# Reordering the opening of a fused cross-attention and feed-forward kernel, and moving small VectorE operations to GpSimd

## The chip, the cores and the metric

The kernel runs on one core of a Trainium2 chip. The metric is the device time of one execution in microseconds (us), lower is better. A core has TensorE (matrix products, called PE in the profile; its weight loads are PEld), VectorE (DVE), ScalarE (ACT), GpSimd (POOL) and SyncE (SP, which here only issues transfers). Each engine works through its own queue in the order in which the program wrote it, and waits on semaphores for the others. PSUM is the memory that TensorE writes; SBUF holds everything else on the chip.

## The reference

`x` has 2048 tokens of 256 numbers, the context 1601 tokens of 192; there are 16 heads of 64, and one learned "null" key and value is put in front of the context's.

```python
x = x + attention(layernorm(x), context, mask, ...)
x = x + ffn(layernorm(x), ...)

def attention(t, context, mask, g_norm, null_kv, Wq, Wkv, Wout, g_out):
    q = (layernorm(t) * g_norm) @ Wq
    k, v = split(context @ Wkv)                    # 16 heads
    k, v = concat(null_k, k), concat(null_v, v)    # 1602 keys
    sim = where(mask, q @ k.T / 8, -max)
    return layernorm(softmax(sim) @ v @ Wout) * g_out

def ffn(h):                                        # weights are +1 or -1
    h = 2 * relu(s0 * (concat(h, -h) @ sign(k0)))  # 512 -> 1024
    h = 2 * relu(s1 * (h @ sign(k1)))              # 1024 -> 1024
    return s2 * (h @ sign(k2))                     # 1024 -> 256
```

## The kernel before

**Units.** Attention is worked in 32 units: 8 pairs of heads (`p`) by 4 blocks of 512 tokens (`b`), with `u` counting them from 0 to 31. The 1602 keys are cut into 13 tiles of 128 (`KC`), the last of which holds 66 (`KLAST`). In a unit, `exps` computes for each key tile the scores of both heads on TensorE (L414), which ScalarE turns into exponentials (L440). In between, `max_chunk` computes the scores of the *next* unit in a faster number format (L373), and VectorE takes their row maxima (L376); twelve chunks of up to 512 keys, and one short chunk `REST` for the last 66 keys (L357, L360). `max_combined` (L381) joins the maxima, `max_turned` transposes them on TensorE (L386) and spreads them on VectorE (L388). They are subtracted in the next unit's first two key tiles (L438).

**Sums of the exponentials.** GpSimd adds the exponentials of the 13 tiles to `acc`, first tiles 1 to 7 while they come (L689, L691), then tile 0, which holds the 66 last keys, and tiles 8 to 12 (L699). Before tile 0 is added or used, ScalarE scales its rows from 64 on with `spent` (L697), a count of masked keys that `masked_counted` works out in unit 0 on VectorE (L400 to L404). TensorE multiplies the exponentials with the values (L447), tile 0 last. In the next unit ScalarE copies one element of the finished `acc` (L680) ahead of the third exponential. So the exponentials from there on, which reuse the buffers, need no further wait for GpSimd.

**Norms of the tokens.** `input_root` takes the statistics of a block on VectorE (L79, L80) and the root on ScalarE (L508); `input_normed` takes the reciprocal (L512), and with `beside` lets ScalarE subtract and scale in eight operations (L145, L146). Root and exponential need different tables on ScalarE, so each change between them is an ACT_TABLE_LOAD. `input_turned` transposes on TensorE and multiplies with the norm weights `gn_sb` (L526 to L530). Blocks 0 and 1 are done in the opening, 2 and 3 at the end of units 0 and 1 (L710 to L712), after the scaling and the sums have been issued.

**The opening** (L548 to L646) is written out by hand: transfers on three queues (SP, ScalarE, GpSimd), idle products on the identity, the first tokens, then for head pair 0 the keys in four chunks (`first_keys`: L230, L231, and L222 on VectorE), the values in four groups of two halves (`first_values`, copied by ScalarE at L295), the queries (`project_q`) and the maxima of unit 0. All of them take PSUM from two pools with two banks each; `slot` takes them from the two pools in turn, so a request is served when the tile that was taken four requests earlier has been read. `keys_stepped` (L272) is GpSimd's: it replaces key tiles by differences, since scores are summed up in PSUM from tile to tile.

**Other small work.** In unit 3 VectorE derives the signs and scales of the feed-forward part from `s0`, `s1`, `s2` (L748 to L752); they are first used in unit 28. In units 1 to 3 it also masks the context (`context_masked`, L407). The feed-forward part follows unit 31.

The order on each engine is the order of the program's text: both parts stand in `tc.manual_schedule()`.

Of the kernel before, what the change touches and what calls it, by code (L numbers as in the profile page):

```python
# [19 lines left out]
M = 1601  # L20
KEYS = M + 1
CD = 192
HEADS, DH = 16, 64
# [15 lines left out]
def xattn_ffn(ctx, tc, x, ctxT, mask, g_norm, null_kv, wq, wkv, wout, g_out, k0, k1, k2, s0, s1, s2, out):  # L39
    nc = tc.nc  # L40
# [3 lines left out]
    sp = ctx.enter_context(tc.tile_pool(name="stats", bufs=2))  # L44
# [10 lines left out]
    x_sb = cp.tile([128, NB * 4, D], F32, name="x_sb")  # L55
    y_sb = cp.tile([128, NB * 4, D], F32, name="y_sb")
    gout_sb = cp.tile([128, D], F32, name="gout_sb")
    s_sb = cp.tile([128, 3], F32, name="s_sb")
# [89 lines left out]
    with ExitStack() as att:  # L148
# [22 lines left out]
        def load_pair(p):  # L171
            wq_t = pp.tile([128, 2, 128], F32, tag="wq", name=f"wq_{p}")
            wa_t = pp.tile([128, 2, 128], F32, tag="wa", name=f"wa_{p}")
            wb_t = pp.tile([128, 2, 128], F32, tag="wb", name=f"wb_{p}")
            wo_t = lp.tile([128, D], F32, tag="wo", name=f"wo_{p}")
            both = wkv.rearrange("r (k w) -> r k w", k=2)[:, :, ts(p, 128)]
            nc.sync.dma_start(out=wa_t, in_=both[0:128])
            nc.sync.dma_start(out=wb_t[:64], in_=both[128:CD])
            if p == 0:

                nc.vector.memset(wb_t[64:], 0.0)
            else:
                nc.sync.dma_start(out=wb_t[64:], in_=both[128:CD])
            nc.sync.dma_start(out=wq_t, in_=wq[:, ts(p, 128)].rearrange("(c r) w -> r c w", c=2))
            if p > 0:
                nc.sync.dma_start(out=wo_t, in_=wout[ts(p, 128), :])
            weights[p] = (wq_t, wa_t, wb_t, wo_t)
# [36 lines left out]
        def first_keys(n, get):  # L224

            kT, _, kr = pairs[0]
            start, w = CHUNKS[n]
            keys = ds(start, w)
            ps = get(f"psk_0_{n}")
            nc.tensor.matmul(ps[:, 0, :w], weights[0][1][:, 0, :], ctx_a[:, keys], start=True, stop=False)  # L230
            nc.tensor.matmul(ps[:, 0, :w], weights[0][2][:, 0, :], ctx_b[:, keys], start=False, stop=True)  # L231

            relative(kT, ps[:, 0, :w], keys)
            if n == 3:
                nc.vector.memset(kT[:, KEYS:], 0.0)
            if n == 0:
                nc.scalar.copy(kr[:, keys], kT[:, keys])
            else:
                nc.gpsimd.tensor_copy(kr[:, keys], kT[:, keys])
# [138 lines left out]
        def max_combined(p, b):  # L378

            cols = mcol.rearrange("p (j c) -> p c j", j=2)[:, 0:4, :]  # L380
            nc.vector.tensor_reduce(cols, maxima[p, b], AX.X, ALU.max, negate=True)  # L381
# [16 lines left out]
        def masked_counted():  # L398

            nc.vector.tensor_reduce(spent, keep[:, 1:], AX.X, ALU.add)  # L400
            nc.vector.tensor_scalar(spent, spent, float(M), None, ALU.subtract)
            nc.vector.tensor_tensor(spent, spent, ident[:, KLAST : KLAST + 1], ALU.mult)
            for row in range(64, KLAST):
                nc.vector.tensor_tensor(spent, spent, ident[:, row : row + 1], ALU.add)  # L404

        def context_masked(part, start, end):
            nc.vector.tensor_tensor(part[:, start:end], part[:, start:end], keep[:, start:end], ALU.mult)  # L407
# [94 lines left out]

        def input_root(b):
            mv = stats(x_sb[:, ts(b, 4), :], 4, f"x{b}")
            r = sp.tile([128, 4], F32, tag="rstd", name=f"rstd_x{b}")
            nc.scalar.activation(r, mv[:, :, 1], AF.Sqrt, bias=eps2_sb, scale=1.0 + EPS)  # L508
            return mv, r

        def input_normed(b, mv, r, beside=False):
            nc.vector.reciprocal(r, r)  # L512
            if beside:
                centred_beside(y_sb, x_sb, mv, r, b)
                return
            for j in range(4):
                centred(y_sb[:, 4 * b + j, :], x_sb[:, 4 * b + j, :], mv, r, j)

        def input_turned(b, get=flex):

            pt = get(f"xT_{b}")
            pts = (pt, (get if b == 0 else spare)(f"xT_{b}_1") if b in (0, 2) else pt)
            for j in range(4):
                for c in range(2):
                    nc.tensor.transpose(pts[c][:, c, ts(j, 128)], y_sb[:, 4 * b + j, ts(c, 128)], ident)
            nc.scalar.mul(xnT[:, b, 0, :], pts[0][:, 0, :], gn_sb[:, 0:1])  # L526
            if b == 1:
                nc.scalar.mul(xnT[:, b, 1, :], pts[1][:, 1, :], gn_sb[:, 1:2])
            else:
                nc.vector.tensor_scalar_mul(xnT[:, b, 1, :], pts[1][:, 1, :], gn_sb[:, 1:2])  # L530
# [7 lines left out]
        def load_x(b):  # L538
            nc.sync.dma_start(out=x_sb[:, ts(b, 4), :], in_=x[ts(b, 512), :].rearrange("(c p) d -> p c d", p=128))

        def load_context(engine, n):
            at, w = CHUNKS[n]
            skip = 1 if n == 0 else 0
            engine.dma_start(out=ctx_a[:, ds(at + skip, w - skip)], in_=ctxT[0:128, ds(at + skip - 1, w - skip)])
            engine.dma_start(out=ctx_b[:64, ds(at + skip, w - skip)], in_=ctxT[128:CD, ds(at + skip - 1, w - skip)])


        nc.gpsimd.memset(keep[:, 0:1], 0)  # L548
        nc.gpsimd.dma_start(out=keep[:, 1:], in_=mask.partition_broadcast(128))
        for t in range(4):  # L550
            (nc.sync, nc.scalar)[t % 2].dma_start(out=x_sb[:, t, :], in_=x[ts(t, 128), :])
        load_context(nc.scalar, 0)
        load_pair(0)
        load_context(nc.sync, 1)
        load_x(1)
        load_context(nc.sync, 2)
        load_context(nc.sync, 3)
        nc.sync.dma_start(out=weights[0][3], in_=wout[ts(0, 128), :])
# [7 lines left out]
        nc.vector.memset(ctx_a[:, KEYS:], 0.0)  # L566
        nc.vector.memset(ctx_b[:64, KEYS:], 0.0)
        nc.vector.memset(ones, 1.0)
        make_identity(nc, ident)
        nc.gpsimd.dma_start(out=gn_sb, in_=g_norm.rearrange("(c p) -> p c", p=128))  # L570
        for j in range(2):
            nc.gpsimd.dma_start(out=nullk[ts(j, DH), :], in_=null_kv[0].rearrange("(p o) -> p o", o=1))
        nc.gpsimd.memset(mcol_u8[0:1, 0:1], 1)
        nc.gpsimd.dma_start(out=mcol_u8[1:128, 0:1], in_=mask[0:127].rearrange("(p o) -> p o", o=1))
        nc.gpsimd.dma_start(
# [20 lines left out]
        input_normed(0, *xn)  # L596

        idle = slot("idle")
        for _ in range(16):
            nc.tensor.matmul(idle[:, 0, :128], ident, ident, start=True, stop=True)  # L600
        input_turned(0, slot)
        first_keys(0, slot)
        project_q(0, 0, slot)

        xn = input_root(1)
        first_keys(1, slot)
        input_normed(1, *xn, beside=True)

        nc.gpsimd.tensor_copy(kept[:, : KC - 1], mcol_u8[:, : KC - 1])
        nc.gpsimd.tensor_copy(kept[:KLAST, KC - 1 : KC], mcol_u8[:KLAST, KC - 1 : KC])  # L610

        max_chunk(0, 0, 0, slot)
        max_chunk(0, 0, 3, slot)
        first_keys(2, slot)
        max_chunk(0, 0, 6, slot)
        max_chunk(0, 0, 9, slot)
        first_values(0, 0, slot)
        first_values(0, 1, slot)

        nc.scalar.activation(warm, eps_sb, AF.Exp)  # L620
        max_chunk(0, 0, 1, slot)
        max_chunk(0, 0, 4, slot)
        first_keys(3, slot)
        keys_stepped(0)
        first_values(1, 0, slot)
        max_chunk(0, 0, 7, slot)
        first_values(1, 1, slot)
        max_chunk(0, 0, 10, slot)
        max_chunk(0, 0, 2, slot)
        input_turned(1, slot)  # L630
        first_values(2, 0, slot)
        max_chunk(0, 0, REST, slot)
        first_values(2, 1, slot)
        max_chunk(0, 0, 5, slot)
        first_values(3, 0, slot)
        max_chunk(0, 0, 8, flex)
        project_q(0, 1, spare, 0)
        max_chunk(0, 0, 11, flex)
        project_q(0, 1, spare, 1)
        max_combined(0, 0)  # L640

        odd = spare("sT_0_0_1")
# [6 lines left out]
        with tc.manual_schedule():  # L649
            for u, (p, b) in enumerate(units):  # L650
# [40 lines left out]
                        nc.gpsimd.tensor_tensor(acc, acc, es[k], ALU.add)  # L691
                if nxt is not None:
                    max_combined(*nxt)
                if u == 0:
                    masked_counted()

# [7 lines left out]
                if u == len(units) - 2:  # L704
# [2 lines left out]
                    norm_end(0, y_sb, y_sb, beside=True)  # L707

                    nc.scalar.activation(warm, eps_sb, AF.Exp)
                if u < 2:  # L710
                    input_normed(u + 2, *input_root(u + 2), beside=True)
                    nc.scalar.activation(warm, eps_sb, AF.Exp)  # L712
                if u == 0:


                    nc.sync.dma_start(out=ctx_b[64:, 1:KEYS], in_=ctxT[128:CD, :])


# [24 lines left out]
                    context_masked(ctx_b, 0, 1024)  # L743
                if u == 3:
                    context_masked(ctx_b, 1024, KEYS)


                    nc.vector.tensor_scalar(sgn, s_sb[:, 0:2], 0.0, None, ALU.is_ge)  # L748
                    nc.vector.tensor_scalar(sgn, sgn, 2.0, -1.0, ALU.mult, ALU.add)
                    nc.vector.tensor_tensor(s_sb[:, 0:2], s_sb[:, 0:2], sgn, ALU.mult)  # L750
                    nc.vector.tensor_scalar(s_out, s_sb[:, 0:1], s_sb[:, 1:2], 8.0, ALU.mult, ALU.mult)
                    nc.vector.tensor_tensor(s_out, s_out, s_sb[:, 2:3], ALU.mult)  # L752
                if p + 1 < NP and b in (1, 2):
                    round_k(p + 1, b - 1)
                avs = lp.tile([128, 512], F32, tag="avs", name=f"avs_{p}_{b}", bufs=1)
# [172 lines left out]
```

## Time and profile before

| what | before |
|---|---|
| median of 3 runs | 1285.53 us (1283.4 to 1285.76) |
| the profiled execution | 1286.19 us |
| its span, first to last instruction | 1284.4 us |
| mean granted TensorE clock | 0.994 |
| busy: TensorE, VectorE, ScalarE, GpSimd | 1264.9, 768.3, 716.8, 1005.9 us |
| first exponential of unit 0 | starts at 38.65 us |
| copy that awaits the sums, units 1, 2, 3, 4 | 76.70, 111.15, 144.67, 184.26 us |

A line of the timeline gives the start in us from the first instruction, the duration in us, the engine, the line of the program, the operation, output and inputs by name with their shapes, and how many instructions are merged in it. In brackets stands the idle time of the engine just before and what ended it. A line of the waits reads: who waited, for whom, us in total, how often, the longest. A line of the windows gives for a stretch of time its length, the busy time of PE, PEld, DVE, ACT and POOL, then the granted clock of TensorE (1.00 is full), the share in which the transfer engines were busy, and GB/s.

### The profile page before, as it was taken

The page shows a single profiled execution, that of the slowest core. Times are in us where ns is not written, and L with a number is a line of the kernel's source. Part 1 is how long each engine was busy: PE and PEld are TensorE (multiplying, and loading weights), DVE is VectorE, ACT ScalarE, POOL GpSimd, SP SyncE. Part 2 cuts the span into 40 slices and gives each one's busy share as a digit, 9 for nine tenths or more (in the row PEclk, how much of TensorE's full clock was granted, in tenths as well). Part 3 has the DMA queues.
Part 4 walks back from the last instruction along what each step waited for, and adds up shares of the span by engine and source line. Part 5 has one row for each costly group of instructions (what it writes and reads, how often), then busy time and mean ns, then how long its engine had stood idle before and what let it go on. Part 6 is the DMA issues. An engine that isn't in the chain of part 4 may idle for free.

```text
span 1284.4 us, 19605 instructions
## 1 busy us (share of the span) xinstructions
PE 1264.9 (98%) x8336; PEld 651.5 (51%) x8336; DVE 768.3 (60%) x831; ACT 716.8 (56%) x974; POOL 1005.9 (78%) x505
## 2 busy tenths in 40 slices
PE   8999989999999999999999999999999999999998
PEld 6334444444444444444444444444444433788887
DVE  6778676656665666565666566656666783644432
ACT  3676645666566656666666666666666666422120
POOL 5688978899889988999889988998899999801100
PEclk9999989999999999999999999999999999999999
DMA  5100000000000000000000000000000010000000
GB/s 145 23 1 5 1 1 13 5 1 1 14 5 1 1 14 5 1 1 14 5 1 1 1 13 5 1 1 5 1 17 1 1 42 1 1 12 6 17 17 17
DMA packets 16169, 13.40 MB, mean 10 GB/s; under 512 B 2689, under 2 KB 15553, under 8 KB 16081
## 3 DMA queue, kind: packets, MB, share of 16 engines
q1 hardware_dynamic: 14944, 11.02, 3.1%
q8 instruction: 65, 1.06, 0.3%
q10 hardware_dynamic: 656, 0.79, 0.2%
q0 software_dynamic: 480, 0.34, 0.2%
q14 instruction: 24, 0.19, 0.0%
HBM read 10.04 MB, written 2.10 MB: 9 GB/s over the span
## 4 chain that ended last, share of the span: by engine, by line
PE 87%; POOL 7%; DVE 2%; ACT 2%; DMA 1%; issue 1%; SPq 0%; DVEq 0%; POOLq 0%; ACTq 0%
PE sT L414 26%; PE av L447 23%; PE ps L810 11%; PE max L373 6%; PE po L460 4%; PE psq L215 4%; POOL acc L699 4%; POOL acc L691 3%; PE ps L841 2%; PE psv L316 2%; PE psk L247 2%; PE psv L328 1%; PE sT L438 1%; PE den L471 1%; PE psk L252 1%; DMA x_sb<-in_x 1%
## 5 line engine op out<-in xcount | busy, mean ns | idle before, releaser
L376 DVE TENSOR_REDUCE mx<-max 128x2 f32<-128x1024 f32 x384 | 444.0, 1219 | 90.2 <-PE max L373 86.4
L699 POOL TENSOR_TENSOR acc<-acc,e 128x1024 f32<-128x1024 f32 x192 | 473.3, 2465 | 16.8 <-ACT e L697 1.8
L440 ACT ACTIVATE e<-sT 128x1024 f32<-128x1024 f32 x416 | 424.9, 1023 | 88.0 <-PE sT L438 45.3
L414 PE MATMUL sT<-qT,kT 64*128 64x512 f32 x1664 | 445.0, 609 | 5.1 <-ACT e L440 5.0
L691 POOL TENSOR_TENSOR acc<-acc,e 128x1024 f32<-128x1024 f32 x160 | 378.9, 2368 | 12.5
L447 PE MATMUL av<-e,v 128*32 128x512 f32 x3328 | 363.6, 592 | 0.0
L373 PE MATMUL max<-kr,qr 64*128 64x512 f32 x768 | 280.8, 719 | 0.8 <-DVE mx L376 0.8
L447 PEld LDWEIGHTS av<-e,v 128*32 128x32 f32 x3328 | 107.6, 110 | 237.5 <-issue 229.9
L414 PEld LDWEIGHTS sT<-qT,kT 64*128 64x128 f32 x1664 | 134.6, 186 | 135.8 <-ACT e L440 123.5
L689 POOL TENSOR_TENSOR acc<-e,e 128x1024 f32<-128x1024 f32 x32 | 75.6, 2361 | 76.5 <-ACT e L440 76.5
L373 PEld LDWEIGHTS max<-kr,qr 64*128 64x128 f32 x768 | 76.7, 188 | 88.9 <-DVE mx L376 66.2
L489 ACT COPY aoT<-r 32x256 f32<-32x256 f32 x224 | 90.2, 403 | 33.5 <-DVE r L483 31.2
L756 ACT COPY avs<-av 128x512 f32<-128x512 f32 x32 | 18.7, 585 | 145.0 <-PE av L447 145.0
L388 DVE TENSOR_TENSOR mT<-mt,pick 128x512 fp32r<-128x512 f32 x32 | 22.1, 691 | 116.9 <-PE mt L386 116.9
L490 DVE TENSOR_TENSOR aoT<-avs,aoT 128x512 f32<-128x512 f32 x28 | 26.9, 961 | 94.3 <-ACT aoT L489 94.3
L810 PE MATMUL ps<-h0hi,w 128*128 128x512 f32 x256 | 79.5, 392 | 0.0
L810 PE MATMUL ps<-h0lo,w 128*128 128x512 f32 x256 | 78.9, 390 | 0.0
L124 POOL TENSOR_TENSOR y_sb<-y_sb,gout_sb 128x256 f32<-128x256 f32 x12 | 9.3, 776 | 86.0 <-DVE y_sb L91 86.0
L216 ACT ACTIVATE qr<-psq 128x512 fp32r<-128x512 f32 x32 | 19.1, 597 | 95.0 <-PE psq L215 92.3
L798 ACT ACTIVATE h1hi<-ps 128x1024 fp32r<-128x1024 f32 x16 | 16.4, 1027 | 98.9 <-PE ps L810 98.9
L215 PE MATMUL psq<-xnT,wq 128*128 128x512 f32 x124 | 59.0, 599 | 2.0 <-ACT xnT L526 2.0
L460 PE MATMUL po<-wo,aoT 128*128 128x256 f32 x256 | 60.6, 380 | 0.0
(170 smaller groups left out, 1199.4 us busy)
## 6 DMA issues: line engine op xcount, KB each, us to landing
out_x<-o SPq DMA_DIRECT2D x7, 256.0 KB, 2.1
x_sb<-in_x SPq DMA_DIRECT2D x3, 512.0 KB, 9.1
wa<-in_wkv SPq DMA_DIRECT2D x8, 128.0 KB, 3.0
wq<-in_wq SPq DMA_DIRECT2D x8, 128.0 KB, 2.2
wo<-in_wout SPq DMA_DIRECT2D x8, 128.0 KB, 2.1
xnT<-in_k SPq DMA_DIRECT2D x1, 1024.0 KB, 5.5
wb<-in_wkv SPq DMA_DIRECT2D x15, 64.0 KB, 2.5
ctx_a<-in_ctxT SPq DMA_DIRECT2D x2, 256.0 KB, 7.3
```

The lines of the kernel that those rows point to most:

```text
L215: nc.tensor.matmul(ps[:, 0, :], weights[p][0][:, c, :], xnT[:, b, c, :], start=c == 0, stop=c == 1)
L373: nc.tensor.matmul(ps[:, j, :w], qr[rows, ts(t, 128)], kr[rows, ds(start, w)], start=True, stop=True)
L376: nc.vector.tensor_reduce(maxima[p, b][:, t, :, c], ps[:, :, :w], AX.X, ALU.max)
L414: nc.tensor.matmul(ps[:n, j, :], kT[rows, ds(128 * KEY_TILES[k], n)], qT[rows, :], start=k < 2, stop=k >= 2, skip_group_check=k >= 2,)
L440: nc.scalar.activation(e, ps, AF.Exp)
L447: nc.tensor.matmul(av[ts(i, 32), 0, :], v[:n, KEY_TILES[k], ts(i, 32)], e[:n, i // 2, :], start=k == 1, stop=k == 0, tile_position=(0, 32 ...
L460: nc.tensor.matmul(pv[:, t, :], aoT[:, ts(t, 128)], weights[p][3], start=True, stop=True)
L489: nc.scalar.copy(aoT[ds(64 * j + 32 * rows, 32), ts(h, 256)], r[ds(64 * j + 32 * h, 32), :])
L689: nc.gpsimd.tensor_tensor(acc, es[1], es[2], ALU.add)
L691: nc.gpsimd.tensor_tensor(acc, acc, es[k], ALU.add)
L699: nc.gpsimd.tensor_tensor(acc, acc, es[k], ALU.add)
L810: nc.tensor.matmul(ps[:, f, :], w(c)[:, ts(2 * g + f, 128)], parts[part][:, c, :], start=i == 0, stop=i == len(steps) - 1,)
```

## The change

It has six parts.

1. GpSimd builds the identity first and issues the transfers of the norm weights `gn_sb` and the null key `nullk` ahead of the mask's.
2. SP loads the second block of tokens ahead of the second chunk of the context.
3. The statistics of block 1 are split: two of its four tiles ahead of the first keys, two behind them; its root goes behind `project_q`, and the rest of its norm behind the first two chunks of maxima. The idle products go from 16 to 11.
4. In the opening, chunks of maxima come ahead of the keys of chunks 1 to 3, and the short chunk `REST` comes last.
5. In units 0 and 1 the norm of blocks 2 and 3 comes ahead of the count of masked keys and of the scaling of tile 0, and so ahead of GpSimd's sums of tiles 0 and 8 to 12.
6. The count's small steps, three instead of four, and the five operations on signs and scales go from VectorE to GpSimd, the latter from unit 3 to unit 4.

```diff
         def masked_counted():
             nc.vector.tensor_reduce(spent, keep[:, 1:], AX.X, ALU.add)
-            nc.vector.tensor_scalar(spent, spent, float(M), None, ALU.subtract)
-            nc.vector.tensor_tensor(spent, spent, ident[:, KLAST : KLAST + 1], ALU.mult)
+            nc.gpsimd.tensor_scalar(spent, spent, float(M), ident[:, KLAST : KLAST + 1], ALU.subtract, ALU.mult)
             for row in range(64, KLAST):
-                nc.vector.tensor_tensor(spent, spent, ident[:, row : row + 1], ALU.add)
+                nc.gpsimd.tensor_tensor(spent, spent, ident[:, row : row + 1], ALU.add)
...
         nc.gpsimd.memset(keep[:, 0:1], 0)
+        make_identity(nc, ident)
+        nc.gpsimd.dma_start(out=gn_sb, in_=g_norm.rearrange("(c p) -> p c", p=128))
+        for j in range(2):
+            nc.gpsimd.dma_start(out=nullk[ts(j, DH), :], in_=null_kv[0].rearrange("(p o) -> p o", o=1))
         nc.gpsimd.dma_start(out=keep[:, 1:], in_=mask.partition_broadcast(128))
...
         load_pair(0)
+        load_x(1)
         load_context(nc.sync, 1)
-        load_x(1)
...
         idle = slot("idle")
-        for _ in range(16):
+        for _ in range(11):
             nc.tensor.matmul(idle[:, 0, :128], ident, ident, start=True, stop=True)
         input_turned(0, slot)
+        mv = stats(x_sb[:, 4:6, :], 2, "x1")
         first_keys(0, slot)
+        stats(x_sb[:, 6:8, :], 2, "x1", mv)
         project_q(0, 0, slot)
-        xn = input_root(1)
-        first_keys(1, slot)
-        input_normed(1, *xn, beside=True)
+        r = input_scale(1, mv)
...
         max_chunk(0, 0, 0, slot)
         max_chunk(0, 0, 3, slot)
-        first_keys(2, slot)
+        input_normed(1, mv, r, beside=True)
+        first_keys(1, slot)
         max_chunk(0, 0, 6, slot)
+        first_values(0, 0, slot)
         max_chunk(0, 0, 9, slot)
-        first_values(0, 0, slot)
         first_values(0, 1, slot)
         nc.scalar.activation(warm, eps_sb, AF.Exp)
         max_chunk(0, 0, 1, slot)
         max_chunk(0, 0, 4, slot)
+        first_keys(2, slot)
+        max_chunk(0, 0, 7, slot)
+        first_values(1, 0, slot)
+        max_chunk(0, 0, 10, slot)
+        first_values(1, 1, slot)
+        max_chunk(0, 0, 2, slot)
         first_keys(3, slot)
         keys_stepped(0)
-        first_values(1, 0, slot)
-        max_chunk(0, 0, 7, slot)
-        first_values(1, 1, slot)
-        max_chunk(0, 0, 10, slot)
-        max_chunk(0, 0, 2, slot)
+        max_chunk(0, 0, 5, slot)
         input_turned(1, slot)
         first_values(2, 0, slot)
-        max_chunk(0, 0, REST, slot)
+        max_chunk(0, 0, 8, slot)
         first_values(2, 1, slot)
-        max_chunk(0, 0, 5, slot)
-        first_values(3, 0, slot)
-        max_chunk(0, 0, 8, flex)
+        max_chunk(0, 0, 11, flex)
         project_q(0, 1, spare, 0)
-        max_chunk(0, 0, 11, flex)
+        first_values(3, 0, flex)
         project_q(0, 1, spare, 1)
+        max_chunk(0, 0, REST, flex)
         max_combined(0, 0)
...
                 if nxt is not None:
                     max_combined(*nxt)
+                if u < 2:
+                    input_normed(u + 2, *input_root(u + 2), beside=True)
+                    nc.scalar.activation(warm, eps_sb, AF.Exp)
                 if u == 0:
                     masked_counted()
...
-                if u < 2:
-                    input_normed(u + 2, *input_root(u + 2), beside=True)
-                    nc.scalar.activation(warm, eps_sb, AF.Exp)
...
-                    nc.vector.tensor_scalar(sgn, s_sb[:, 0:2], 0.0, None, ALU.is_ge)
-                    nc.vector.tensor_scalar(sgn, sgn, 2.0, -1.0, ALU.mult, ALU.add)
-                    nc.vector.tensor_tensor(s_sb[:, 0:2], s_sb[:, 0:2], sgn, ALU.mult)
-                    nc.vector.tensor_scalar(s_out, s_sb[:, 0:1], s_sb[:, 1:2], 8.0, ALU.mult, ALU.mult)
-                    nc.vector.tensor_tensor(s_out, s_out, s_sb[:, 2:3], ALU.mult)
+                if u == 4:
+                    nc.gpsimd.tensor_scalar(sgn, s_sb[:, 0:2], 0.0, None, ALU.is_ge)
+                    nc.gpsimd.tensor_scalar(sgn, sgn, 2.0, -1.0, ALU.mult, ALU.add)
+                    nc.gpsimd.tensor_tensor(s_sb[:, 0:2], s_sb[:, 0:2], sgn, ALU.mult)
+                    nc.gpsimd.tensor_scalar(s_out, s_sb[:, 0:1], s_sb[:, 1:2], 8.0, ALU.mult, ALU.mult)
+                    nc.gpsimd.tensor_tensor(s_out, s_out, s_sb[:, 2:3], ALU.mult)
```

`input_scale(b, mv)` is new: it takes the two lines of `input_root` that take the root of the variances on ScalarE.

More of the change, by code (lines that the diff above doesn't have):

```diff
@@ L500, in divided, with input_scale @@
             return aoT
+        def input_scale(b, mv):
+            r = sp.tile([128, 4], F32, tag="rstd", name=f"rstd_x{b}")
+            nc.scalar.activation(r, mv[:, :, 1], AF.Sqrt, bias=eps2_sb, scale=1.0 + EPS)
+            return r
         def input_root(b):
             mv = stats(x_sb[:, ts(b, 4), :], 4, f"x{b}")
-            r = sp.tile([128, 4], F32, tag="rstd", name=f"rstd_x{b}")
-            nc.scalar.activation(r, mv[:, :, 1], AF.Sqrt, bias=eps2_sb, scale=1.0 + EPS)
-            return mv, r
+            return mv, input_scale(b, mv)
         def input_normed(b, mv, r, beside=False):
@@ L568, in xattn_ffn @@
         nc.vector.memset(ones, 1.0)
[L569 to L572, printed above, removed]
         nc.gpsimd.memset(mcol_u8[0:1, 0:1], 1)
```

## The prediction

> **What bounds the kernel now.** I read the page's totals first, then who waited for whom in the first units, and then each engine's timeline there, because the change touches only the opening and the units 0 to 4.
>
> ```profile
> PE 1264.9 (98%) x8336; PEld 651.5 (51%) x8336; DVE 768.3 (60%) x831; ACT 716.8 (56%) x974; POOL 1005.9 (78%) x505
> ...
> PE psv L316 <- DVE mT L388: 3.9, 1, 3.9
> PE psq L215 <- ACT xnT L526: 2.0, 1, 2.0
> ```
>
> TensorE is busy 98% of the span, so a gain can only come out of its few holes. The second view (waits of TensorE between 38 and 250 us) names the two of over 1 us behind the opening. The first, 3.9 us, is at the end of unit 3. This is VectorE's timeline there:
>
> ```profile
> 168.02 2.31 DVE L748 TENSOR_SCALAR sgn<-s_sb 128x2 f32<-128x2 f32 x1
> 170.37 0.17 DVE L749 TENSOR_SCALAR sgn<-sgn 128x2 f32<-128x2 f32 x1
> 170.58 2.19 DVE L750 TENSOR_TENSOR s_sb<-s_sb,sgn 128x2 f32<-128x2 f32 x1
> ...
> 173.05 2.13 DVE L752 TENSOR_TENSOR s_out<-s_out,s_sb 128x1 f32<-128x1 f32 x1
> 175.10 0.68 DVE L388 TENSOR_TENSOR mT<-mt,pick 128x512 fp32r<-128x512 f32 x1
> ```
>
> Three tiny operations take over 2 us each while GpSimd adds, and the turned maxima (L388) stand behind them. The second hole is ScalarE's, at the end of unit 0; then come GpSimd's sums:
>
> ```profile
> 52.40 1.02 ACT L440 ACTIVATE e<-sT 128x1024 f32<-128x1024 f32 x1 [0.28 <-PE sT L414]
> 57.20 1.15 ACT L697 ACTIVATE e<-e,spent 64x1024 f32<-64x1024 f32 x1 [3.78 <-DVE spent L404]
> 58.37 1.28 ACT L508 ACT_TABLE_LOAD   x1
> ...
> 66.68 0.69 ACT L526 ACTIVATE xnT<-xT,gn_sb 128x512 f32<-128x512 f32 x1
> ```
>
> ```profile
> 58.49 14.54 POOL L699 TENSOR_TENSOR acc<-acc,e 128x1024 f32<-128x1024 f32 x6 [1.79 <-ACT e L697]
> 77.97 2.37 POOL L689 TENSOR_TENSOR acc<-e,e 128x1024 f32<-128x1024 f32 x1 [4.94 <-ACT e L440]
> ```
>
> The reader is to see the order on ScalarE: last exponential, scaling of the last key tile (L697), then the norm of later tokens. GpSimd's last six sums start with the tile that L697 scales. In the next unit a one-element copy on ScalarE (L680) waits for the last of them, and every later exponential is queued behind it:
>
> ```profile
> 76.70 0.17 ACT L680 COPY seen<-acc 1x1 f32<-1x1 f32 x1
> 76.87 1.02 ACT L440 ACTIVATE e<-sT 128x1024 f32<-128x1024 f32 x1
> ```
>
> The sums ended at 58.49 + 14.54 = 73.03, so L680 had 3.67 us to spare. In unit 2 it stands at 111.15 and the sums (16.40 us from 92.65) ended at 109.05: 2.10 us to spare. Last, the clock and the opening:
>
> ```profile
> 17.46:20.88 3.42, 2.03 (x10) 1.01 (x10) 3.42 (x7) 2.84 (x8) 0.87 (x3) 1.00 1.09 313
> 20.88:24.29 3.41, 3.41 (x17) 2.81 (x15) 2.27 (x3) 1.68 (x5) 0.65 (x2) 0.50 0.18 46
> ```
>
> ```profile
> 11.96 0.75 DVE L222 SCALAR_TENSOR_TENSOR kT<-psk,nullk,keep 128x512 f32<-128x512 f32 x1 [1.08 <-PE psk L231]
> 14.93 0.43 DVE L79 BATCH_NORM_STATS2 st_x<-x_sb 128x6 f32<-128x256 f32 x1 [2.22 <-DMA x_sb<-in_x]
> ```
>
> A stretch of 3.4 us in which TensorE was busy only 2.03 us is followed by one at a granted clock of 0.50. And VectorE, which works in order, sat 2.22 us until the second tokens landed.
>
> **The change part by part.** The profiled execution took 1286.19 us (span 1284.4), 0.66 over the median of the three runs. Sums are made on its rows.
>
> *Unit 3's five operations.* They leave VectorE for GpSimd one unit later. In unit 3 TensorE transposed the maxima at 168.16; 0.37 later (so in unit 2) L388 could start: 168.53. From L388 to the next L680 an undisturbed unit of this kind takes 316.31 - 307.33 = 8.98 us, so L680 would stand at 177.51, and stands at 184.26: 6.75 us, 3.90 of it the hole, the rest work at clock 0.50 (174.5 to 181.3). GpSimd's sums of unit 3 end at 177.59, so 0.1 comes back: **-6.65** (ends -3.9, if only the hole counts, and -6.75). On GpSimd the five cost about 0.21 us each (the 128x4 addition of the opening, L589), 1.05 us; that they are behind unit 4's sums and ahead of unit 5's, where GpSimd idled 3.1 us, covers it. If that cover were gone it would be 1.05 us once. What reads them runs in unit 28 and after.
>
> *Unit 0: the norm ahead of the scaling.* Also the count of masked keys ends on GpSimd: three operations of 0.2 us for VectorE's 0.15, 0.70 and twice 0.16. In the new order ScalarE loads its table at 53.45 instead of idling. VectorE's statistics (2.2 us from 53.98) end at 56.2, root, reciprocal and mean follow by 56.9, eight ScalarE operations as at 92.79 to 96.67 (3.88) end at 60.8, the table back and its first use at 62.2. Only then the scaling, 62.2 to 63.35; the count (reduction 1.8 from 56.9, then GpSimd's 0.6) is ready at 59.5 and no longer matters. TensorE wants the scaled tile at 62.95 and waits 0.45. Its transposes and their copy follow with 0.7 of idling, and the projection L215 starts at 66.15 instead of 67.43; with no drop of the clock its 3.95 us (1.72 + 1.35 + 0.88, as around 210) put the first scores of unit 1 at 70.1 instead of 73.16. That is a gain of 3.06, and it isn't kept: GpSimd's six sums start at 63.45 instead of 58.49 and end at 78.0. L680 would be ready at 76.70 - 3.06 = 73.64 and waits 4.4 us. Behind it are the exponentials, behind them TensorE's scores, two tiles on. Unit 1's third exponential starts at 78.17, where it started at 76.87: **+1.3**, less 0.2 that TensorE wins back by steps of 1.09 instead of 1.13.
>
> *The clock after that wait.* TensorE idles some 4.4 us. Holes of 2.20 us (64.8 to 67.43) and 3.90 cost 1.78 (5.73 instead of 3.95 us up to the scores) and 2.85 more at half clock. How much falls on work depends on where the hole lies against the 3.4 us stretches: between 0 and 2.85, taken as **+2.0**, between the two rows.
>
> *Unit 1: the same order.* Here ScalarE did not idle ahead of L697, so nothing is gained. The scaling, at 89.46, goes behind the norm: 98.1 to 99.25. GpSimd's six sums, which began at 92.65, begin at 99.3 and at unit 0's 14.54 end at 113.85; L680 of unit 2 was at 111.15: **+2.7**, however late unit 1 runs as a whole. Less 0.3 won back, and **+1.8** of clock (ends 0 and 2.85; taken at the 2.20 us hole's 1.78, the nearest). TensorE itself wants unit 1's scaled tile at 100.1, after 99.25. In unit 2 the scaling stays where it was and GpSimd's delay dies: its sums end at about 148.8, L680 comes at 152.
>
> [...]
>
> *The opening.* The norm weights land earlier (10.03 before), but the query projection also waits for its weights, which landed at 11.03: nothing. Five idle products fewer (ten matmuls of 0.213 us) let the transposes run when the tokens are ready, but the first keys' matmuls wait for weights that land at 9.8: nothing. The mask, issued behind the identity and three small transfers on GpSimd, lands about 2 us later than 7.88, before the first keys at 11.96. On SP the second tokens pass two context transfers. Before, those tokens took 2.18 us behind what preceded them (12.73 to 14.91); behind the query weights (11.03) they land at about 13.2, and the context at about 14.9, where the second keys now need it at 17.2. But VectorE now has half the statistics *ahead of* the first keys' L222: 13.2, two pairs of 0.53 to 14.3, L222 to 15.1 (before: 12.7), its copy on ScalarE to 15.75, the scaled queries behind it to 16.35. The maxima's matmuls start then (15.23 before), their reductions at 16.95 (17.84 before). Then in turn: two reductions 2.28, reciprocal and mean 0.25, eight ScalarE operations 3.88, the copy of the first values 0.58 (queued behind them), at 24.0; keys 2 reuse that bank and start at 24.2. Before, at 24.46 TensorE had done all of this and keys 2 as well (1.72). From 24.46 to L438 at 38.11 it worked through 13.65 us; now 24.2 + 13.65 + 1.72, and 0.3 because the short last chunk's reduction (0.71) and the combination come behind everything: 39.85. **+1.7**. Ends: tokens landed by the time of the first keys, -0.6 (the chain begins 2.4 earlier); tokens no earlier than before, +3.4.
>
> Sum: -6.65 + 1.3 - 0.2 + 2.0 + 2.7 - 0.3 + 1.8 + 1.7 = +2.35. Forecast **1286.19 + 2.35 = 1288.5 us**. About 0.2% of the time, 2.57 us, is what a measurement of this kernel can tell from no change: slower begins at 1288.1, faster at 1282.96.
>
> **The rivals.**
> *Nobody waits for GpSimd (faster).* If its sums were through by the time of L680, unit 0 would keep 3.06 and unit 1 lose nothing: 1286.19 - 6.65 - 3.06 + 1.7 = 1278.2. It decides if the scaling of unit 0 ends by 59.0 (L680 at 73.64 less 14.54). For it: GpSimd is idle in 22% of the span. Against: each unit's slack is 0.8 to 2.5 us in the later units, and L680 already waits 4.0 us in units 29 to 31.
> *The clock holds through both waits.* 2.35 - 3.8: 1284.7. For it: a hole cut by the edge of a stretch may stay under what drops it. Against: three of three holes over 1.4 us dropped it.
> *The opening gains.* With -0.6 for +1.7: 1286.2. It needs the tokens by 10.9; against it stands 11.03 for the weights queued ahead of them.
> *Larger loss.* Tokens as late as before (+1.7 more) and clock losses at their ends (+1.9): 1292.1.
>
> **How the numbers follow.** Forecast 0.45, own range 1286.5 to 1291; nobody waits 0.15; clock holds 0.12; opening gains 0.15; larger loss 0.13. Faster: 0.15 and 0.05 for the two 'no change' rivals together (1282.4). Slower: three quarters of the forecast, 0.33, and 0.13. Same: the rest, 0.34. The range leaves out most of the 1278 case below and little above: 1281.5 to 1293.
>
> **What would show it.** L680 waiting 4 to 5 us in unit 1 and 2 to 3.5 in unit 2 for GpSimd's L699, with TensorE's holes of that size and a granted clock of 0.50 behind them; no wait on L388 in unit 3; the statistics of the second tokens ending at about 14.3 ahead of L222; the first exponential at about 40.4 instead of 38.65. Wrong if L680 finds its sum ready, or if the opening ends before 38.

## The result and the profile after

Over 22 executions each, the changed kernel takes 1286.8 us in the median (1284.67 to 1289.03) and the kernel before 1284.2 us (1281.85 to 1286.64). The ratio is 1.0019, 95% interval 1.0013 to 1.0026: 2.4 us slower, just inside the 0.2% that the prediction called no change. It had forecast +2.35 us and gave a clear loss 0.46, no clear change 0.34.

Both kernels spread by over 4 us, and the two profiled executions lie at opposite ends. That of before took 1286.19 us at a mean granted clock of 0.994, that of the changed kernel 1284.84 us at 0.999. Among the 22 changed executions those at 0.999 took 1284.7 and 1284.8 us, those at 0.993 took 1288.5 and 1289.0. The spread goes with the granted clock, and the two profiles show where theirs differ: their last microseconds aside, four stretches of 3.41 us at 0.50 before (from 20.88, 68.66, 174.48 and 177.89), one in the changed kernel (from 78.56). So medians are compared below, and profiles only for the waits, the clock and the distances between operations.

The page's first row and the waits of TensorE in the first 250 us (who waited, for whom, us in total, times, longest):

```profile
PE 1261.0 (98%) x8326; PEld 646.9 (50%) x8326; DVE 757.4 (59%) x822; ACT 717.0 (56%) x974; POOL 1006.2 (78%) x513
...
PE sT L413 <- ACT e L439: 7.0, 3, 3.9
PE max L373 <- ACT qr L216: 1.9, 1, 1.9
...
PE psk L230 <- ACT v L295: 1.1, 1, 1.1
```

Of the two holes named before, the wait for the spread maxima in unit 3 is gone, and 0.6 us is left of the projection's 2.0. New ones have come: TensorE's scores now wait 7.0 us for exponentials. The timeline of ScalarE and GpSimd at the end of unit 0 and in unit 1 says why (L703 is the scaling, L705 the last six sums, L683 the copy that awaits them; in brackets the idle time ahead):

```profile
61.76 1.14 ACT L703 ACTIVATE e<-e,spent 64x1024 f32<-64x1024 f32 x1
62.98 14.53 POOL L705 TENSOR_TENSOR acc<-acc,e 128x1024 f32<-128x1024 f32 x6 [3.96 <-ACT e L703]
77.55 0.19 ACT L683 COPY seen<-acc 1x1 f32<-1x1 f32 x1 [4.15 <-POOL acc L705]
...
101.80 14.56 POOL L705 TENSOR_TENSOR acc<-acc,e 128x1024 f32<-128x1024 f32 x6 [8.50 <-ACT e L703]
116.39 0.19 ACT L683 COPY seen<-acc 1x1 f32<-1x1 f32 x1 [2.81 <-POOL acc L705]
```

The scaling went from 57.20 to 61.76, behind the norm, and the sums from 58.49 to 62.98. The copy, which found its sum ready at 76.70 before, now idles 4.15 us until 77.55. In unit 1 GpSimd idles 8.50 us for the scaling and ends at 101.80 + 14.56 = 116.36; the copy of unit 2 idles 2.81 us for it. Over the whole span the copy waited 4.0 us in three units before, and now, by the view of its tile:

```profile
  POOL acc L705: 11.0, 5
```

What a wait does behind itself is seen in two neighbouring stretches (length; busy time of PE, PEld, DVE, ACT, POOL; granted clock, transfer share, GB/s):

```profile
75.14:78.56 3.42, 0.00 (x0) 0.00 (x0) 0.96 (x1) 1.01 (x2) 2.34 (x1) 1.00 0.00 0
78.56:81.97 3.41, 3.27 (x12) 1.64 (x12) 0.72 (x1) 2.02 (x3) 3.16 (x2) 0.50 0.00 0
```

In unit 3 the spread maxima (L388) wait only for TensorE's transposition, and the five moved operations stand in GpSimd's queue in unit 4:

```profile
173.67 0.69 DVE L388 TENSOR_TENSOR mT<-mt,pick 128x512 fp32r<-128x512 f32 x1 [0.35 <-PE mt L386]
...
213.73 0.23 POOL L748 TENSOR_SCALAR sgn<-s_sb 128x2 f32<-128x2 f32 x1
...
214.97 0.19 POOL L752 TENSOR_TENSOR s_out<-s_out,s_sb 128x1 f32<-128x1 f32 x1
216.86 2.37 POOL L692 TENSOR_TENSOR acc<-e,e 128x1024 f32<-128x1024 f32 x1 [1.70 <-ACT e L439]
```

They span 1.43 us, and GpSimd still idles 1.70 us behind them. The three operations that took over 2 us each on VectorE (L748, L750, L752 before) take about 0.2 us each here.

In the opening, the second tokens are there at 11.4 instead of 14.9, yet keys 2 wait for the copy of the first values (L79 is the first statistics of these tokens, L222 the first keys, L373 the first maxima, which wait for the scaled queries of L216, L230 keys 2, and L439 the first exponential):

```profile
11.40 0.43 DVE L79 BATCH_NORM_STATS2 st_x<-x_sb 128x6 f32<-128x256 f32 x1 [2.47 <-DMA x_sb<-in_x]
12.60 0.75 DVE L222 SCALAR_TENSOR_TENSOR kT<-psk,nullk,keep 128x512 f32<-128x512 f32 x1
14.55 0.74 PE L373 MATMUL max<-kr,qr 64*128 64x512 f32 x4 [1.94 <-ACT qr L216]
22.02 1.13 PE L230 MATMUL psk<-ctx_a,wa 128*128 128x512 f32 x2 [1.12 <-ACT v L295]
...
38.18 1.94 ACT L439 ACTIVATE e<-sT 128x1024 f32<-128x1024 f32 x2 [1.76 <-PE sT L437]
```

### The profile page after: what moved, and what is told of

The parts are those of the page before. It is cut to its first block, busy times and chain, and to the rows that moved or that the text cites. A ratio compares the mean times of both kernels' runs of the same rounds, so it can differ in the third digit from the quotient of the medians.

```text
span 1283.1 us, 19580 instructions
## 1 busy us (share of the span) xinstructions
PE 1261.0 (98%) x8326; PEld 646.9 (50%) x8326; DVE 757.4 (59%) x822; ACT 717.0 (56%) x974; POOL 1006.2 (78%) x513
## 4 chain that ended last, share of the span: by engine, by line
PE 86%; POOL 9%; ACT 2%; DVE 1%; issue 1%; DMA 1%; DVEq 0%; SPq 0%; POOLq 0%
PE sT L413 25%; PE av L446 24%; PE ps L810 11%; PE max L373 6%; POOL acc L705 6%; PE po L459 4%; PE psq L215 3%; POOL acc L694 3%; PE ps L841 2%; PE psv L316 2%; PE psk L247 1%; PE den L470 1%; PE psv L328 1%; PE sT L437 1%; ACT e L439 1%; PE max L357 1%
## 5 line engine op out<-in xcount | busy, mean ns | idle before, releaser
L705 POOL TENSOR_TENSOR acc<-acc,e 128x1024 f32<-128x1024 f32 x192 | 471.3, 2455 | 27.4 <-ACT e L703 12.5
L439 ACT ACTIVATE e<-sT 128x1024 f32<-128x1024 f32 x416 | 424.9, 1024 | 88.2 <-PE sT L437 43.6
L694 POOL TENSOR_TENSOR acc<-acc,e 128x1024 f32<-128x1024 f32 x160 | 379.2, 2370 | 12.6
L373 PE MATMUL max<-kr,qr 64*128 64x512 f32 x768 | 281.3, 720 | 1.9 <-ACT qr L216 1.9
L373 PEld LDWEIGHTS max<-kr,qr 64*128 64x128 f32 x768 | 76.7, 187 | 90.5 <-DVE mx L376 63.4
L388 DVE TENSOR_TENSOR mT<-mt,pick 128x512 fp32r<-128x512 f32 x32 | 22.1, 691 | 116.6 <-PE mt L386 116.6
L216 ACT ACTIVATE qr<-psq 128x512 fp32r<-128x512 f32 x32 | 19.1, 598 | 92.6 <-PE psq L215 91.4
L799 DVE SCALAR_TENSOR_TENSOR h1lo<-ps,h1hi 128x1024 fp32r<-128x1024 f32 x16 | 19.6, 1224 | 67.7 <-ACT h1hi L798 67.7
```

Source lines behind the costliest of these rows:

```text
L373: nc.tensor.matmul(ps[:, j, :w], qr[rows, ts(t, 128)], kr[rows, ds(start, w)], start=True, stop=True)
L439: nc.scalar.activation(e, ps, AF.Exp)
```

## The experiments

The theory: the new order of norm and scaling makes the next unit's copy wait for GpSimd, in units 1 and 2, and each wait costs half clock besides; the signs' move gains what it takes off VectorE; the opening loses a little. The rivals: the loss is in the opening alone; the signs' stall is replaced by another; the clock falls on time that is lost anyway. The kernel before ran beside each set, with medians of 1284.56 (the first four), 1283.83 (the next four) and 1284.99 us (the last).

### One part at a time

**Signs alone**, on the kernel before:

```diff
-                    nc.vector.tensor_scalar(sgn, s_sb[:, 0:2], 0.0, None, ALU.is_ge)
+                if u == 4:
+                    nc.gpsimd.tensor_scalar(sgn, s_sb[:, 0:2], 0.0, None, ALU.is_ge)
...
```

> The kernel before with one part of the change: the five operations on signs and scales on GpSimd in unit 4. Theory (the stall on VectorE in unit 3 was real and nothing takes its place): the wait of 3.9 us on the spread maxima in unit 3 is gone, with the half clock behind it, so 5.9 to 6.65 us less than before, a ratio of 0.9948 to 0.9954. Rival (GpSimd's sums of unit 3, which end at 177.6, are what is late next): the copy in unit 4 waits 2 us or more for them, and the gain is under 4 us, a ratio over 0.9969.

1278.11 us, ratio 0.9950 (0.9938 to 0.9963): 6.45 us less. The copy of unit 4 is the first thing that is late next, by next to nothing:

```profile
177.71 0.19 ACT L680 COPY seen<-acc 1x1 f32<-1x1 f32 x1
```

It stood at 184.26 before; GpSimd's sums end at 177.67, 0.04 us ahead of it. The rival falls. Three tiny operations, of over 2 us each on VectorE beside GpSimd's sums, cost half a per cent of the kernel.

**Norm order alone**, on the kernel before:

```diff
                 if nxt is not None:
                     max_combined(*nxt)
+                if u < 2:
+                    input_normed(u + 2, *input_root(u + 2), beside=True)
+                    nc.scalar.activation(warm, eps_sb, AF.Exp)
                 if u == 0:
                     masked_counted()
...
-                if u < 2:
-                    input_normed(u + 2, *input_root(u + 2), beside=True)
-                    nc.scalar.activation(warm, eps_sb, AF.Exp)
```

> The kernel before with one part of the change: the norm of blocks 2 and 3 ahead of the count, the scaling and the sums. Theory: the copy waits 4 to 5 us for the sums in unit 1 and 2.5 to 3 us in unit 2, with half clock behind, 5 to 9 us more than before, a ratio of 1.004 to 1.007. Rival (ScalarE's idle time at the end of unit 0 is worth more than the waits): a ratio under 1.

1291.84 us, ratio 1.0054 (1.0041 to 1.0066): 7.28 us more. The view of the copy's tile shows the same waits as the changed kernel, 10.9 us in five units where the kernel before had 4.0 in three:

```profile
  POOL acc L702: 10.9, 5
```

The gain at the end of unit 0 is there as well (TensorE's wait for the projection is 0.6 us instead of 2.0), and nothing of it is left behind the copy, which waits 4.12 us in unit 1.

**Opening alone**, on the kernel before: parts 1 to 4 of the change.

```diff
+        make_identity(nc, ident)
+        nc.gpsimd.dma_start(out=gn_sb, in_=g_norm.rearrange("(c p) -> p c", p=128))
...
         nc.gpsimd.dma_start(out=keep[:, 1:], in_=mask.partition_broadcast(128))
...
+        load_x(1)
         load_context(nc.sync, 1)
-        load_x(1)
...
+        mv = stats(x_sb[:, 4:6, :], 2, "x1")
         first_keys(0, slot)
+        stats(x_sb[:, 6:8, :], 2, "x1", mv)
...
```

> The kernel before with the new opening alone (its transfers, its order, 11 idle products). Forecast's step: the statistics of the second tokens hold up the first keys, 1.7 us more, a ratio of 1.0013. Reading of the profile after: the second tokens land at 11.4 instead of 14.9, and the first exponential starts 0.5 us earlier, so a ratio of 0.9996, no difference that can be told.

1283.95 us, ratio 0.9998 (0.9989 to 1.0007): nothing that can be told. The interval reaches from -1.4 to +0.9 us, so a loss of 1.7 is excluded here. But this execution's profile shows the first exponential at 40.11, later than in the kernel before (38.65), and the reason is a hole of 3.1 us for the scaled queries with two stretches at half clock behind it:

```profile
10.80:14.23 3.43, 0.73 (x2) 0.00 (x0) 2.62 (x8) 0.77 (x2) 1.28 (x6) 1.00 0.95 191
14.23:17.64 3.41, 3.01 (x6) 1.34 (x7) 2.42 (x4) 1.02 (x3) 0.20 (x2) 0.50 0.70 231
17.64:21.05 3.41, 3.41 (x9) 1.46 (x8) 1.78 (x5) 2.95 (x7) 0.61 (x1) 0.50 0.98 260
```

**Norm order undone** in the changed kernel:

```diff
-                if u < 2:
-                    input_normed(u + 2, *input_root(u + 2), beside=True)
-                    nc.scalar.activation(warm, eps_sb, AF.Exp)
                 if u == 0:
                     masked_counted()
...
+                if u < 2:
+                    input_normed(u + 2, *input_root(u + 2), beside=True)
+                    nc.scalar.activation(warm, eps_sb, AF.Exp)
```

> The changed kernel with one part undone: the norm of blocks 2 and 3 again behind the scaling and the sums. Theory (the changed order makes the next unit's copy wait for GpSimd): no wait of the copy for the sums in units 1 and 2, and 6 to 9 us less than the changed kernel, about 1278 us, a ratio to the kernel before of 0.994 to 0.996. Rival (the waits are hidden by what unit 0 gains, the loss is in the opening): no faster than the changed kernel, a ratio of 1.001 or more.

1279.28 us, ratio 0.9957 (0.9944 to 0.9969), 7.5 us less than the changed kernel by the medians. The copy waits 4.0 us in three units, as before, and TensorE's 2.0 us wait for the projection is back. This kernel differs from signs alone by the opening (and by the three small steps of the count on GpSimd, which no run prices by themselves). It is 1.17 us slower in the same set, but the ranges of the two overlap (1278.09 to 1280.4 and 1277.02 to 1279.91), so that this difference is not clear.

The parts add up within their uncertainty: signs -6.45, norm order +7.28 alone or +7.5 in place, opening between -0.3 alone and +1.2 on top of the signs; the sum lies between +0.5 and +2.3, measured +2.4 (1.7 to 3.3).

### The two waits and the clock

**Unit 1's norm put back, unit 0's left ahead:**

```diff
-                if u < 2:
+                if u < 1:
                     input_normed(u + 2, *input_root(u + 2), beside=True)
...
+                if u == 1:
+                    input_normed(u + 2, *input_root(u + 2), beside=True)
+                    nc.scalar.activation(warm, eps_sb, AF.Exp)
```

> The changed kernel with the norm of block 3, in unit 1, again behind the sums; that of block 2, in unit 0, stays ahead. Theory: the copy's wait of 2.8 us in unit 2 goes, and the half clock that follows it in most executions, so 2.5 to 4.5 us less than the changed kernel, 1282.3 to 1284.3 us; the wait of 4.1 us in unit 1 stays. Rival (only the longer wait counts, unit 2's is made up by later slack): within 1 us of the changed kernel.

1282.79 us, ratio 0.9991 (0.9983 to 1.0000), 4.0 us less than the changed kernel. TensorE is left with one wait of over 1 us, the 3.9 us in unit 1:

```profile
PE sT L413 <- ACT e L439: 3.9, 1, 3.9
PE psq L215 <- ACT xnT L528: 0.6, 1, 0.6
```

The rival falls: unit 2's wait of 2.8 us cost 4.0 by the medians, 3.6 by the two ratios, whose intervals together leave 2.2 to 5.0. So the times alone do not show that it cost more than itself; the distances under the next run do. What is left of the norm order's price, about 3.5 us, is unit 0's.

**Both holes filled.** The waits stay, but TensorE multiplies the identity with itself in them:

```diff
                     if nxt is not None:
                         max_chunk(*nxt, order[k])
+                    if k == 3 and u in (1, 2):
+                        fill = flex(f"fill_{u}")
+                        for _ in range(16 if u == 1 else 10):
+                            nc.tensor.matmul(fill[:, 0, :128], ident, ident, start=True, stop=True)
```

> The changed kernel with idle products on the identity behind the fourth chunk of maxima in units 1 and 2, 16 (3.4 us) and 10 (2.2 us), so that TensorE is busy while the copy waits for the sums. The waits of 4.1 and 2.8 us themselves stay. Theory (each wait costs about 2 us more by the half clock behind it): no stretch at 0.50 in units 1 and 2, and 2 to 4 us less than the changed kernel, 1283 to 1285 us. Rival (the half clock falls on time in which TensorE would wait anyway): no difference to the changed kernel beyond 1 us.

1283.74 us, ratio 0.9995 (0.9984 to 1.0005), 3.1 us less than the changed kernel. The copy still waits (10.9 us in five units), and no stretch in units 1 and 2 is at half clock:

```profile
75.30:78.70 3.40, 3.19 (x26) 2.29 (x23) 2.69 (x3) 0.00 (x0) 3.32 (x2) 1.00 0.00 0
78.70:82.10 3.40, 3.40 (x27) 2.74 (x27) 0.02 (x1) 2.25 (x4) 2.18 (x2) 1.00 0.00 0
...
116.40:119.80 3.40, 3.40 (x28) 2.53 (x26) 0.65 (x2) 2.61 (x4) 2.18 (x2) 1.00 0.00 0
```

So the half clock behind the two waits is worth about 3 us (the intervals of the two ratios together leave 1.5 to 4.7), and it is not time that TensorE would have waited anyway. The distances in the profiles agree. From unit 1's copy to unit 2's it is 34.45 us in the kernel before, 37.38 with the holes filled, and 38.84 in the changed kernel, where a stretch of 3.41 us at half clock lies between them: the wait of 2.8 us costs 2.9, the stretch 1.5. From unit 2's copy to unit 3's it is 33.42 in the changed kernel, where no half clock followed, and 34.82 with the norm order alone, where one stretch did: 1.4.

### What the transfers do in the opening

**Mask first:** the changed kernel with the mask's 200 KB ahead of the identity, the norm weights and the null key again; SP's order stays the new one.

```diff
+        nc.gpsimd.dma_start(out=keep[:, 1:], in_=mask.partition_broadcast(128))
         make_identity(nc, ident)
...
-        nc.gpsimd.dma_start(out=keep[:, 1:], in_=mask.partition_broadcast(128))
```

> The changed kernel with the mask's transfer issued first on GpSimd again, ahead of the identity, the norm weights and the null key. Theory (the mask's 200 KB, no longer ahead, is what let the second tokens land at 11.4 instead of the forecast's 13.2): they land at 12.8 to 13.3, the first keys' operation on VectorE goes from 12.6 to about 14, and the first exponential starts 1 to 2 us later than in the changed kernel, 1287.5 to 1289 us. Rival (the place in SP's queue alone sets the landing): they land at 11.0 to 11.7 and the time is that of the changed kernel within 0.5 us.

1289.89 us, ratio 1.0042 (1.0027 to 1.0057), 3.1 us more than the changed kernel. VectorE's timeline:

```profile
13.40 0.43 DVE L79 BATCH_NORM_STATS2 st_x<-x_sb 128x6 f32<-128x256 f32 x1 [2.78 <-DMA x_sb<-in_x]
...
14.60 0.75 DVE L222 SCALAR_TENSOR_TENSOR kT<-psk,nullk,keep 128x512 f32<-128x512 f32 x1
```

The tokens land at 13.4 (11.2 to 11.6 in the six other profiles with the new order), the query projection's weights a microsecond later than in the changed kernel (10.52 instead of 9.48), and the first exponential is at 41.56. The rival falls: the place in SP's queue alone does not bring the tokens to 11.4. In this profile the first exponential is 3.4 us later than in the changed kernel's, more than the 2 us of the landing, and the hole in front of the maxima has become 3.9 us, with two stretches at half clock behind it:

```profile
15.10:18.52 3.42, 1.97 (x5) 1.00 (x6) 2.39 (x6) 1.79 (x4) 0.00 (x0) 0.50 0.92 306
18.52:21.93 3.41, 3.41 (x6) 0.96 (x4) 1.77 (x5) 1.94 (x5) 0.00 (x0) 0.50 0.69 168
```

### A version that beats both

If the scaling must not be late and ScalarE's idle time at the end of unit 0 is the count's fault, the count belongs somewhere else. In the opening VectorE idles while the second tokens land. **Early count**, on the changed kernel with the norm order undone:

```diff
         def masked_counted():
-            nc.vector.tensor_reduce(spent, keep[:, 1:], AX.X, ALU.add)
...
         input_turned(0, slot)
+        nc.vector.tensor_reduce(spent, keep[:, 1:], AX.X, ALU.add)
         mv = stats(x_sb[:, 4:6, :], 2, "x1")
...
         nc.gpsimd.tensor_copy(kept[:KLAST, KC - 1 : KC], mcol_u8[:KLAST, KC - 1 : KC])
+        masked_counted()
...
-                if u == 0:
-                    masked_counted()
```

> The changed kernel with the norm of blocks 2 and 3 behind the scaling and the sums as before, and the count of masked keys in the opening: its reduction on VectorE just ahead of the statistics of the second tokens, its small steps on GpSimd behind the copy of the mask's columns. Theory: in unit 0 ScalarE scales right behind the last exponential, at about 53, so neither it nor GpSimd waits; the projection at the end of unit 0 starts 1.5 us earlier than with the norm simply put back, without the half clock, so 2.5 to 3.5 us less than that version's 1279.3, 1275.8 to 1276.8 us, a ratio of 0.993 to 0.994. Rival (the count was no limit, ScalarE's norm is): no difference to 1279.3 beyond 1 us.

1275.91 us, ratio 0.9937 (0.9924 to 0.9950). On ScalarE nothing stands between the last exponential and the scaling:

```profile
52.06 1.02 ACT L438 ACTIVATE e<-sT 128x1024 f32<-128x1024 f32 x1 [0.28 <-PE sT L412]
53.12 1.15 ACT L699 ACTIVATE e<-e,spent 64x1024 f32<-64x1024 f32 x1
54.28 1.28 ACT L505 ACT_TABLE_LOAD   x1
```

GpSimd's sums start at 56.4, when its own earlier sums are through, and end 1.8 us ahead of the copy. TensorE's only waits over 0.2 us between 38 and 250 us are 0.6 and 0.5. From the first exponential to unit 1's copy it is 34.51 us here and 38.47 with the norm order undone, whose projection has a stretch at half clock behind its wait. The whole is 3.4 us less than that version by the medians, 2.6 by the ratios, and the rival falls by the distance. This keeps what the norm order was after at the end of unit 0, without its price.

**Early count with the old opening:** the kernel before, signs moved, the reduction ahead of `input_root(1)`, where VectorE idled 2.2 us:

```diff
+        nc.vector.tensor_reduce(spent, keep[:, 1:], AX.X, ALU.add)
         xn = input_root(1)
         first_keys(1, slot)
```

> The same early count and the signs on GpSimd, but with the opening of before (the count's reduction in VectorE's idle time ahead of the second tokens' statistics). Together with the version with the new opening it prices the opening once more. If the new opening gains the 0.5 us that the two profiles show: 0.3 to 0.8 us slower than that version. If half clock in the new opening's hole costs 1.7 us in half of the executions: 0 to 1 us faster.

1275.05 us, ratio 0.9931 (0.9918 to 0.9943), the fastest here: 8.8 us less than the kernel before, most of it the signs' 6.45, and 11 to 12 less than the changed one. Against the same count with the new opening it is 0.86 us faster, though the intervals of the two ratios overlap. Neither profile has a stretch at half clock ahead of its last microseconds. The first exponential with the new opening, then with the old one:

```profile
38.32 1.94 ACT L438 ACTIVATE e<-sT 128x1024 f32<-128x1024 f32 x2 [1.76 <-PE sT L436]
...
37.36 1.94 ACT L438 ACTIVATE e<-sT 128x1024 f32<-128x1024 f32 x2 [1.59 <-PE sT L436]
```

These 0.96 us are as much as the whole difference. So this pair does not show the clock cost that the expectation offered as the reason; it points to the new opening's own work being longer.

## Why the prediction was right

**Sum and sign.** +2.35 us forecast, +2.4 measured by the ratio. The forecast of 1288.5 started from a profiled execution 2 us over the median that 22 runs give, so the time itself is 1.7 under it. That the sums agree to 0.1 us is in part luck: the opening's +1.7 was not found (-0.3 alone, and its interval excludes 1.7), and the measured +2.4 is itself known to about 0.8 us. The two large terms are not luck: signs moved, and norm order, whose parts in the forecast add up to +7.3 and which measured +7.28 alone.

**Signs, -6.65.** Measured -6.45. The 0.1 us that the copy was to lose to GpSimd's sums did not come: they end 0.04 us ahead of it. The rival size of 3.9, the hole without its half clock, is excluded by the interval (-8.0 to -4.8).

**Unit 0's norm order.** Every step is found 0.5 us earlier, as the whole opening is: scaling 61.76 (forecast 62.2), sums until 77.51 (78.0), the copy's wait 4.15 (4.4). TensorE's wait for the scaled tile is 0.41 (0.45), the projection starts at 65.72 (66.15).

**Unit 1's norm order.** Wait of 2.81 against 2.7. The argument that this wait does not depend on how late unit 1 runs holds in four profiles with unit 1 at different places: 2.81, 2.79, 2.78, 2.82.

**The clock, +2.0 and +1.8.** 3.1 together instead of 3.8, by the filled holes. The forecast said that the cost depends on where a hole lies. In the profile after, unit 2's hole was followed by no half clock at all; with the mask first and with the norm order alone it was, for 3.4 us. Behind unit 1's hole it lasted 3.4 us in two profiles and 6.8 in two. The stretches here are 3.41 us long and lie differently in the profiles: one begins at 17.46 before, at 17.64 in the opening alone and at 18.52 with the mask first. Unit 2's hole, 2.6 us on TensorE, was followed by half clock in two of three profiles.

**The opening, +1.7.** The step that was off is the landing of the second tokens: forecast at 13.2, found at 11.4. I kept the query weights' landing at 11.03 and put the tokens' 2.18 us behind it, though the mask's 200 KB, which I had noted as two microseconds later, then no longer stood ahead of both. The query weights landed at 9.48 and the tokens 1.90 behind them. With the mask first the tokens land at 13.4, as worked out. So moving the mask alone, on GpSimd's queue, moved these landings on SP's queue, the query weights' from 9.48 to 10.52 and the tokens' from 11.4 to 13.4; by what way is not shown. The rest of the chain held: from the tokens through statistics, first keys, maxima, norm and the copy of the first values to keys 2 it gave 24.2, and with 1.8 less 22.4; found 22.02. Adding the forecast's 13.65, 1.72 and 0.3 gives 37.7; L437, the end of that chain, starts at 37.64. So the term was to be about -0.5 in an execution without half clock there, and its range's lower end (-0.6) says that. Measured, the opening is -0.3 (-1.4 to +0.9) alone and +0.9 to +1.2 in the two pairs with signs moved, neither of them clear of the scatter. That gap comes in part from the old opening: in profiles without half clock there its first exponential is at 37.36 and 37.64, with it at 38.65 and 38.71; the new one has 37.99 to 38.32 without and 40.07 and 40.11 with. Like for like the new opening is later by some 0.4 to 0.9, or 1.4. How often each has the half clock these eleven profiles do not settle. So two of the prediction's signs were not seen: the statistics ended at 12.6 instead of 14.3 ahead of L222, and the first exponential came at 38.18, not at about 40.4. The prediction had also named an opening that ends before 38 as a sign of being wrong. L437 starts at 37.64, so this term was wrong.

**The rival 'nobody waits for GpSimd'** fell at the place that the prediction named: the scaling would have had to end by 59.0, and begins at 61.76. 'The clock holds' fell with the filled holes, though in the profile after it did hold behind unit 2's. 'The opening gains' happened by its mechanism (tokens near 10.9), though with no gain that can be measured.

## What to carry to other kernels

When an operation is moved ahead in one engine's queue, ask what is behind it on that queue, who waits for that, and how much slack the last waiter has. Here a small scaling fed 14.5 us of sums on another engine with 2 to 4 us to spare, and the idle time won on ScalarE (3.78 us in front of the scaling) came back as idle time of TensorE (3.9 us in unit 1, 2.6 in unit 2). If an engine idles in front of a late input, make the input early rather than filling the gap with work that then stands in the way: the early count took 1275.91 us, the changed kernel 1286.8. A transfer's landing was not set by its own queue alone here: with the mask's 200 KB issued first on GpSimd's queue, the tokens on SP's landed at 13.4 instead of 11.4. So list what is issued ahead on the other queues too.

## What the runs showed that was not expected

Cut into the 3.41 us stretches of each execution's clock, its first and last microseconds aside, the eleven profiles order themselves by TensorE's busy time in a stretch. All 17 stretches with 1.49 us or less were followed by one at 0.50. Of the 16 at full clock with 1.60 to 2.03 us only two were, so that the prediction's "three of three holes over 1.4 us" is too strong; of those with 2.09 us or more none was. Behind stretches that were themselves at half clock it was otherwise: those with 2.56, 2.97 and 3.01 us busy were followed by another at 0.50 (the last is the 14.23 row under "Opening alone"), one with 2.90 was not. So in these profiles a summed idle time of 1.9 us or more in a stretch at full clock had a drop behind it every time. With 1.4 to 1.8 us it had one twice in 16: 1.4 us in two holes did (the prediction's 17.46 row), 1.8 us in the changed kernel's stretch from 1037.70 (1.62 us busy) did not.

In unit 1, VectorE's masking of the context (1602 elements) took 4.00 us beside GpSimd's sums before, and 1.82 us in the changed kernel, where GpSimd was idle; the product ahead of it took 2.00 and 0.69. GpSimd's six sums took 16.40 us in unit 1 of the kernel before, beside these two, and 14.56 in the changed kernel, without them.
